# One bank per half for the first row of blocks of a seven-product GRU, and its moving sums in 256-column instructions

## The chip, the cores and the metric

The kernel runs on one core of one Trainium2 chip. The metric is the device time of one execution in microseconds. Kernels are compared by the median of several executions; a profile is one further execution, recorded by the hardware profiler.

## What is computed

Two graph layers run over 128 graphs of 128 nodes with 256 features, all in fp32. Layer 0 is a gated graph network: three steps with shared GRU weights. Layer 1 is one head of graph attention. Each is applied to a normalised input and added to it:

```python
h = jnp.maximum(_layernorm(x, axis=-1), 0.0)
for i in range(3):                       # layer 0
    m = jnp.einsum('bnd,de->bne', h, weight[i])
    aggr = jnp.einsum('bst,bsd->btd', A, m)
    gi = aggr @ w_ih.T + b_ih
    gh = h @ w_hh.T + b_hh
    r = jax.nn.sigmoid(i_r + h_r)
    z = jax.nn.sigmoid(i_z + h_z)
    n = jnp.tanh(i_n + r * h_n)
    h = (1.0 - z) * n + z * h
...
att = softmax(where(adj == 0, -inf, leaky_relu(s1[:, :, None] + s2[:, None, :])))   # layer 1
out = x + einsum('bij,bjo->bio', att, h @ W.T)
```

`gi` and `gh` are split in three parts (r, z, n), and `A` is `adj != 0`. The weights of `m` are multiplied into those of `gi` ahead of the steps, so that a step only aggregates `h` and applies the gates.

## The kernel before

**Tiles.** Four graphs make a group (G = 4), so there are 32 groups and 32 x 3 = 96 GRU steps. The state of a group is kept in columns: tile `hT` is [128 partitions, C = 2 chunks of features, T = 512 columns], where a column is a node. `aT` is the aggregated input in the same form. H = 256 is half of the columns.

**A step** (`gru_step`, L627) has two blocks: `blocks(0, ...)` makes the gate r and the hidden part of n, `blocks(1, ...)` the gate z and the given part of n. A block multiplies a 2 x 2 matrix of weight blocks (output half o, input half) by a 2 x 2 matrix of data blocks X11, X21 (first half of the columns, chunks 0 and 1) and X12, X22 (second half). It does so with seven products instead of eight, after Winograd. `moving_sums` (L441, instructions at L445, L448, L450 and L452) prepares the sums of data on VectorE, once for `hT` and once for `aT`: T1 = X12 - X11, T2 = X22 - T1, T3 = X22 - X12 and T4 = X22 - X21 - T1. The sums of weights S1 to S4 are made once per kernel.

`blocks` (L662) emits in this order, where each product (L636, matmul at L650) is three matmuls of 256 columns, each in two passes of TensorE:

1. `u` = W11 X11, which ScalarE copies to the first halves of `c1` (L670);
2. `m7` = S3 T3, which ScalarE copies to `m` (L673);
3. `u` += S2 T2, after which VectorE makes `c2 = u + m` (L676);
4. the first halves of `c1` += W12 X21, which completes C11;
5. `u` += S1 T1, which ScalarE copies to the second halves of `c1` (L680), and from which VectorE makes `c22 = u + m` (L684); only then is `u` free for the next block;
6. `c2` += N22 T4;
7. the second halves of `c1` += S4 X22, which completes C12.

`c1`, `c2`, `u` and `m7` are in PSUM. `c1` is [128, 2, 512]: one bank for each of the block's two results (q = 0, 1), in which the first half of the columns (C11) and the second (C12) stand side by side. Row o = 0 of the outcome is read from it, both halves in one instruction of 512 columns: r by `reset` (tanh, L701), the hidden part by `state_half` (L708), z by `update` (L734), all on ScalarE, and the given part by `add_half` on VectorE (L741, v += c1). Row o = 1 lies in `c2` and `c22` and is read in instructions of 256 columns at the same lines. `candidate` (L598) then makes v = (r + 1) v, and `state` (L606 to L614) a tanh and three sums on VectorE for each chunk, which give the new `hT`.

**Other work.** `gathered` (L566) multiplies by the adjacency (`pa`) or by the attention (`pq`); `to_rows` (L483) transposes on TensorE. `epilogue` (L803) is the attention of a finished group: norm statistics (L406), scores (`junk`, L840), softmax (L883 to L899), the product with `W` (`po`, L944) and the final sum (L951). For all but the last two groups it turns its tiles by VectorE transposes and small DMAs (`tq`, L827; `prT`). All DMAs are issued from SP (L60).

**What sets the order.** The order on each engine is fixed when the program is built. A planner (class `Order`, L169) keeps a time for each engine at which it is free; every piece of work is a generator that yields an engine, a length and the time at which its inputs are ready. `product` puts its matmuls and then calls `fill`, which issues what fits on the other engines until the product's end, and `matmuls`, which adds up to 1 us of other TensorE work. `finish` runs what must be done first. Two groups are in work alternately (lanes), and `gru_step` returns its two `state` tasks, which the next step, of the other lane, finishes at `order.finish(last)`, after the sixth product of its second block. Lengths that the planner takes are constants in the code. At run time [...] each engine works its list off in order.

Of the kernel before, what the change touches and what calls it, by code (L numbers as in the profile page):

```python
# [14 lines left out]
P = 128  # L15
# [12 lines left out]
def preln_gnn_kernel(  # L28
# [110 lines left out]
    c1 = ps_sum.tile([P, 2, T], F32, name="c1")  # L139
# [3 lines left out]
    for bank in (c1[:, 0, :], c1[:, 1, :], c2.rearrange("p g t -> p (g t)")):  # L143
        put(nc.tensor.matmul(bank, zero[:, 0:P], zero, start=True, stop=True))
# [294 lines left out]
    T1, D1, T2, T4, T3 = range(5)  # L439

    def moving_sums(X, into, ready, name):  # L441

        yield DVE2, 0.36, ready
        t = work.tile([P, 5, H], F32, tag=f"t{name[0]}", name=f"t_{name}")
        put(nc.vector.tensor_tensor(t[:, T3, :], X[:, 1, H:T], X[:, 0, H:T], ALU.subtract))  # L445
        into[T3] = t, order.free[DVE]
        into[T1] = t, (yield DVE2, 0.62, ready)
        put(nc.vector.tensor_tensor(t[:, T1 : D1 + 1, :], X[:, :, H:T], X[:, :, 0:H], ALU.subtract))  # L448
        into[T2] = t, (yield DVE2, 0.36, ready)
        put(nc.vector.tensor_tensor(t[:, T2, :], X[:, 1, H:T], t[:, T1, :], ALU.subtract))  # L450
        into[T4] = t, (yield DVE2, 0.36, ready)
        put(nc.vector.tensor_tensor(t[:, T4, :], t[:, D1, :], t[:, T1, :], ALU.subtract))  # L452
# [174 lines left out]
    def gru_step(s, last):  # L627
# [34 lines left out]
        def blocks(no, gates):  # L662

            m = gate.tile([P, 2, H], F32, tag="m", name=f"m_{name}_{no}")
            c22 = gate.tile([P, 2, H], F32, tag="c22", name=f"c22_{name}_{no}")
            done = product(gates, lambda q: u[:, q, :], W11, (0, 0), None, banks["u"], True, (ACT,))
            t = order.take(ACT, 0.57, max(done, banks["c1"]))
            put(nc.scalar.copy(c1[:, :, 0:H], u))  # L670
            done = product(gates, lambda q: m7[:, q, :], S3, None, T3, 0.0, True, (ACT,))
            tm = order.take(ACT, 0.57, done)
            put(nc.scalar.copy(m, m7))  # L673
            done = product(gates, lambda q: u[:, q, :], S2, None, T2, t, False, (DVE,))
            t = order.take(DVE, 0.62, max(done, tm, banks["c2"]))
            put(nc.vector.tensor_tensor(c2, u, m, ALU.add))  # L676
            product(gates, lambda q: c1[:, q, 0:H], W12, (1, 0), None)
            done = product(gates, lambda q: u[:, q, :], S1, None, T1, t, False, (ACT,))
            t = order.take(ACT, 0.57, done)
            put(nc.scalar.copy(c1[:, :, H:T], u))  # L680

            order.fill(t, (DVE,))
            tc22 = banks["u"] = order.take(DVE, 0.62, t)
            put(nc.vector.tensor_tensor(c22, u, m, ALU.add))  # L684
            done = product(gates, lambda q: c2[:, q, :], N22, None, T4, 0.0, False, (ACT, DVE))
            yield c22, tc22, done
            done = product(
                gates, lambda q: c1[:, q, H:T], S4, (1, 1), None, t, False, (ACT, DVE)
            )
            yield c22, tc22, done  # L690
# [3 lines left out]
        c22, t22, done = next(phase)  # L694
# [4 lines left out]
        def reset(o, cols, src, length, ready):  # L699
            t = order.take(ACT, length, ready)  # L700
            put(nc.scalar.activation(  # L701
                r[:, o, cols], src, AF.Tanh, bias=brz[:, o : o + 1], scale=0.5
            ))
            return t

        def state_half(o, cols, src, length, ready):
            t = order.take(ACT, length, ready)
# [4 lines left out]

        low, high, full = slice(0, H), slice(H, T), slice(0, T)
        reset(1, high, c22[:, 0, :], 0.38, t22)
        reset(1, low, c2[:, 0, :], 0.38, done)
        banks["c2"] = state_half(1, low, c2[:, 1, :], 0.38, done)
        _, _, done = next(phase)
        reset(0, full, c1[:, 0, :], 0.6, done)
        banks["c1"] = state_half(0, full, c1[:, 1, :], 0.6, done)
        t1 = state_half(1, high, c22[:, 1, :], 0.38, t22)  # L720
        s.v_ready = [0.0, 0.0]
        half_task = order.add(0, candidate(s, r, v, (banks["c1"], t1)))
# [3 lines left out]
        c22, t22, done = next(phase)  # L726
# [5 lines left out]
        def update(o, cols, src, length, ready):  # L732
            t = order.take(ACT, length, ready)
# [5 lines left out]
        def add_half(o, cols, src, length, ready):  # L739
            t = order.take(DVE, length, max(ready, s.v_ready[o]))  # L740
            put(nc.vector.tensor_tensor(v[:, o, cols], v[:, o, cols], src, ALU.add))  # L741
            return t

        add_half(1, high, c22[:, 1, :], 0.38, t22)
        update(1, high, c22[:, 0, :], 0.38, t22)
        tv = add_half(1, low, c2[:, 1, :], 0.38, done)
        banks["c2"] = update(1, low, c2[:, 0, :], 0.38, tv)
# [336 lines left out]
```

## Time and profile before

| | us |
|---|---|
| median of 3 runs | 2203.93 (2202.45 to 2205.67) |
| the profiled execution | 2205.54 |
| its span, first to last instruction | 2203.8 |
| TensorE (PE) busy | 2176.6 |
| VectorE (DVE) busy | 1744.5 |
| ScalarE (ACT) busy | 1309.3 |
| GpSimd (POOL) busy | 103.3 |
| mean granted clock of TensorE | 0.997 of full speed |

A group line of the profile names the source line, engine, operation, output <- inputs with their sizes, and the count, then busy us and mean ns of one, then the engine's idle time before and what ended it. A line of the waits names who waited for whom, us in total, times, and the longest. A line of the timeline has the start, the length, the engine and the instruction, with the idle time before it in brackets. Ends of matmuls are modelled: two passes in a row look as if they overlapped, so distances are taken between starts. "c" stands for all of `c1`, `c2`, `c22`, because numbers are left out of names.

### The profile page before, as it was taken

What the parts mean: (1) busy time and instruction counts of PE and PEld (TensorE: products, weight loads), DVE (VectorE), ACT (ScalarE), POOL (GpSimd) and SP (SyncE); (2) the same over time, 40 slices, a digit from 0 to 9 for tenths busy, and PEclk for the clock granted to TensorE, in tenths of its full rate; (3) what the DMA queues carried; (4) which work ended last, traced back from release to release, by engine and by line L of the source; (5) the groups of instructions that cost most, each with busy time, mean ns of one, the idle gap of its engine ahead of it and who ended that gap; (6) DMA issues with size and microseconds to landing.
All of it is one profiled execution on the core that took longest, in us unless ns stands there. A gap on an engine that the chain in (4) does not pass through costs nothing.

```text
span 2203.8 us, 32865 instructions
## 1 busy us (share of the span) xinstructions
PE 2176.6 (99%) x11259; PEld 1931.5 (88%) x11259; DVE 1744.5 (79%) x3960; ACT 1309.3 (59%) x2694; POOL 103.3 (5%) x204
## 2 busy tenths in 40 slices
PE   8999999999999999999999999999999999999997
PEld 7888888888888888888888888888888888888886
DVE  7678777788788878787888787887787888887866
ACT  5566656556566566656566565665655665656654
POOL 1000000000000000000000000000000000000000
PEclk9999999999999999999999999999999999999998
DMA  4001130131212212022210312213022021221101
GB/s 134 1 15 30 30 67 11 31 76 21 56 33 56 48 32 50 25 55 51 52 31 29 61 41 54 53 22 71 20 53 45 20 58 37 56 44 36 33 20 34
DMA packets 380936, 93.24 MB, mean 42 GB/s; under 512 B 325216, under 2 KB 376672, under 8 KB 380768
## 3 DMA queue, kind: packets, MB, share of 16 engines
q1 hardware_dynamic: 380768, 91.13, 19.1%
q8 instruction: 89, 1.46, 0.3%
q14 instruction: 79, 0.65, 0.1%
HBM read 35.92 MB, written 16.84 MB: 24 GB/s over the span
## 4 chain that ended last, share of the span: by engine, by line
PE 91%; DVE 4%; SPq 3%; DMA 1%; ACT 1%; issue 1%; DVEq 0%; ACTq 0%
PE u L650 31%; PE c L650 31%; PE m L650 10%; PE pa L566 7%; PE po L944 4%; SPq L60 3%; PE pq L566 3%; PE pr L483 2%; DMA xt<-in_x 1%; PE pw L348 1%; DVE v L741 1%; ACT z L734 0%; DVE c L684 0%; DVE hT L610 0%; DVE hT L608 0%
## 5 line engine op out<-in xcount | busy, mean ns | idle before, releaser
L650 PE MATMUL u<-t_h,s_hh 128*128 128x256 f32 x1152 | 343.5, 380 | 2.0 <-ACT c L670 2.0
L650 PE MATMUL u<-t_a,s_f 128*128 128x256 f32 x1152 | 311.3, 379 | 0.0
L650 PE MATMUL c<-aT,s_f 128*128 128x256 f32 x1152 | 311.3, 379 | 0.0
L680 ACT COPY c<-u 128x512 f32<-128x512 f32 x192 | 109.4, 570 | 325.8 <-PE u L650 294.3
L650 PEld LDWEIGHTS c<-aT,s_f 128*128 128x128 f32 x1152 | 218.9, 190 | 29.7
L650 PEld LDWEIGHTS u<-t_a,s_f 128*128 128x128 f32 x1152 | 218.9, 190 | 29.7
L650 PEld LDWEIGHTS u<-t_h,s_hh 128*128 128x128 f32 x1152 | 211.9, 190 | 33.8 <-ACT c L670 4.3
L741 DVE TENSOR_TENSOR v<-v,c 128x256 f32<-128x256 f32 (+1 forms) x288 | 139.5, 509 | 126.5 <-ACT z L734 121.5
L734 ACT ACTIVATE z<-c,brz 128x256 f32<-128x256 f32 (+1 forms) x288 | 159.8, 556 | 116.5 <-DVE c L684 67.4
L650 PE MATMUL c<-hT,s_hh 128*128 128x256 f32 x768 | 228.5, 379 | 0.0
L676 DVE TENSOR_TENSOR c<-u,m 128x512 f32<-128x512 f32 x192 | 134.3, 700 | 114.6 <-PE u L650 98.8
L701 ACT ACTIVATE r<-c,brz 128x256 f32<-128x256 f32 (+1 forms) x288 | 151.2, 552 | 91.8 <-DVE c L684 61.8
L684 DVE TENSOR_TENSOR c<-u,m 128x512 f32<-128x512 f32 x192 | 131.8, 687 | 69.2 <-ACT c L680 67.9
L673 ACT COPY m<-m 128x512 f32<-128x512 f32 x192 | 112.6, 587 | 100.4 <-PE m L650 100.4
L650 PE MATMUL m<-t_h,s_hh 128*128 128x256 f32 x576 | 171.5, 379 | 0.0
L650 PE MATMUL c<-t_h,s_hh 128*128 128x256 f32 x576 | 171.4, 379 | 0.0
L670 ACT COPY c<-u 128x512 f32<-128x512 f32 x192 | 111.3, 580 | 85.7 <-DVE v L741 71.9
L650 PEld LDWEIGHTS c<-hT,s_hh 128*128 128x128 f32 x768 | 144.7, 190 | 19.0
L590 ACT COPY aT<-pa 128x512 f32<-128x512 f32 x192 | 109.2, 584 | 84.6 <-PE pa L566 84.5
L650 PE MATMUL m<-t_a,s_f 128*128 128x256 f32 x576 | 156.1, 380 | 0.7 <-DVE t_a L445 0.7
L650 PE MATMUL u<-aT,s_f 128*128 128x256 f32 x576 | 155.6, 379 | 0.0
L650 PE MATMUL c<-t_a,s_f 128*128 128x256 f32 x576 | 155.6, 379 | 0.0
(122 smaller groups left out, 4188.0 us busy)
## 6 DMA issues: line engine op xcount, KB each, us to landing
xt<-in_x SPq DMA_DIRECT2D x31, 512.0 KB
out<-xt SPq DMA_DIRECT2D x31, 512.0 KB
tq<-hT SPq DMA_DIRECT2D x480, 32.0 KB
hT_a<-tq_a SPq DMA_DIRECT2D x448, 32.0 KB
at<-in_adj SPq DMA_DIRECT2D x32, 256.0 KB
e<-line SPq DMA_DIRECT2D x30, 256.0 KB
prT<-e SPq DMA_DIRECT2D x480, 16.0 KB
line<-turned SPq DMA_DIRECT2D x120, 0.5 KB
```

The source lines that it names most:

```text
L566: put(nc.tensor.matmul(pa[:, k * P : (k + 1) * P], h[:, k, c * P : (c + 1) * P], A[:, k, :], start=True, stop=True,))
L590: put(nc.scalar.copy(aT[:, c, :], pa))
L650: put(nc.tensor.matmul(to(q), S[0][:, gate_no, weight, :], moving, start=first and q == 0 and i == 0, stop=(i == len(ends) - 1), skip_grou ...
L670: put(nc.scalar.copy(c1[:, :, 0:H], u))
L673: put(nc.scalar.copy(m, m7))
L676: put(nc.vector.tensor_tensor(c2, u, m, ALU.add))
L680: put(nc.scalar.copy(c1[:, :, H:T], u))
L684: put(nc.vector.tensor_tensor(c22, u, m, ALU.add))
L701: put(nc.scalar.activation(r[:, o, cols], src, AF.Tanh, bias=brz[:, o : o + 1], scale=0.5))
L734: put(nc.scalar.activation(z[:, o, cols], src, AF.Tanh, bias=brz[:, C + o : C + o + 1], scale=0.5))
L741: put(nc.vector.tensor_tensor(v[:, o, cols], v[:, o, cols], src, ALU.add))
L944: put(nc.tensor.matmul(po[:, j, :], hs[:, c, k * P : (k + 1) * P], gwt[:, c, :], start=(c == 0), stop=(c == C - 1),))
```

## The change

`c1` becomes two PSUM tiles of one bank each, by half of the columns: `c1[0]` holds C11 and `c1[1]` holds C12, for both results. `blocks` yields once more, after the fourth product, and `c1[0]` is read there; `c1[1]` is read after the seventh. All reads of row o = 0 are 256 columns now. For the second half, the sum on VectorE stands ahead of the tanh of z. `order.finish(last)` and `order.finish([half_task])` come after the fourth product instead of the sixth. In `moving_sums` T4 is made as T2 - X21, D1 = X22 - X21 is gone, and the four sums are instructions of 256 columns in the order T3, T1, T2, T4. The planner's lengths for them are 0.34, and 0.38 for every read.

```diff
@@ -136,11 +136,12 @@
 
     zero = borrowed(gate, [P, C, T], "r", "zero", T, bufs=1).bitcast(mybir.dt.bfloat16)[:, 0:T]
     put(nc.vector.memset(zero, 0.0))
-    c1 = ps_sum.tile([P, 2, T], F32, name="c1")
+    c1 = [ps_sum.tile([P, 2, H], F32, name=f"c1_{n}") for n in range(2)]
     c2 = ps_sum.tile([P, 2, H], F32, name="c2")
     u = ps_sum.tile([P, 2, H], F32, name="u")
     m7 = ps_sum.tile([P, 2, H], F32, name="m7")
-    for bank in (c1[:, 0, :], c1[:, 1, :], c2.rearrange("p g t -> p (g t)")):
+    for bank in (*c1, c2):
+        bank = bank.rearrange("p g t -> p (g t)")
         put(nc.tensor.matmul(bank, zero[:, 0:P], zero, start=True, stop=True))
...
 
-    T1, D1, T2, T4, T3 = range(5)
+    T1, T2, T3, T4 = range(4)
 
     def moving_sums(X, into, ready, name):
 
-        yield DVE2, 0.36, ready
-        t = work.tile([P, 5, H], F32, tag=f"t{name[0]}", name=f"t_{name}")
-        put(nc.vector.tensor_tensor(t[:, T3, :], X[:, 1, H:T], X[:, 0, H:T], ALU.subtract))
-        into[T3] = t, order.free[DVE]
-        into[T1] = t, (yield DVE2, 0.62, ready)
-        put(nc.vector.tensor_tensor(t[:, T1 : D1 + 1, :], X[:, :, H:T], X[:, :, 0:H], ALU.subtract))
-        into[T2] = t, (yield DVE2, 0.36, ready)
-        put(nc.vector.tensor_tensor(t[:, T2, :], X[:, 1, H:T], t[:, T1, :], ALU.subtract))
-        into[T4] = t, (yield DVE2, 0.36, ready)
-        put(nc.vector.tensor_tensor(t[:, T4, :], t[:, D1, :], t[:, T1, :], ALU.subtract))
+        t = work.tile([P, 4, H], F32, tag=f"t{name[0]}", name=f"t_{name}")
+        x11, x21, x12, x22 = (X[:, c, n * H : (n + 1) * H] for n in range(2) for c in range(2))
+        for i, one, other in ((T3, x22, x12), (T1, x12, x11), (T2, x22, t[:, T1]), (T4, t[:, T2], x21)):
+            into[i] = t, (yield DVE2, 0.34, ready)
+            put(nc.vector.tensor_tensor(t[:, i, :], one, other, ALU.subtract))
...
@@ -666,18 +662,19 @@
             m = gate.tile([P, 2, H], F32, tag="m", name=f"m_{name}_{no}")
             c22 = gate.tile([P, 2, H], F32, tag="c22", name=f"c22_{name}_{no}")
             done = product(gates, lambda q: u[:, q, :], W11, (0, 0), None, banks["u"], True, (ACT,))
-            t = order.take(ACT, 0.57, max(done, banks["c1"]))
-            put(nc.scalar.copy(c1[:, :, 0:H], u))
+            t = order.take(ACT, 0.57, max(done, banks["c1_0"]))
+            put(nc.scalar.copy(c1[0], u))
             done = product(gates, lambda q: m7[:, q, :], S3, None, T3, 0.0, True, (ACT,))
             tm = order.take(ACT, 0.57, done)
             put(nc.scalar.copy(m, m7))
             done = product(gates, lambda q: u[:, q, :], S2, None, T2, t, False, (DVE,))
             t = order.take(DVE, 0.62, max(done, tm, banks["c2"]))
             put(nc.vector.tensor_tensor(c2, u, m, ALU.add))
-            product(gates, lambda q: c1[:, q, 0:H], W12, (1, 0), None)
+            done = product(gates, lambda q: c1[0][:, q, :], W12, (1, 0), None)
+            yield done
             done = product(gates, lambda q: u[:, q, :], S1, None, T1, t, False, (ACT,))
-            t = order.take(ACT, 0.57, done)
-            put(nc.scalar.copy(c1[:, :, H:T], u))
+            t = order.take(ACT, 0.57, max(done, banks["c1_1"]))
+            put(nc.scalar.copy(c1[1], u))
 
             order.fill(t, (DVE,))
             tc22 = banks["u"] = order.take(DVE, 0.62, t)
@@ -685,75 +682,81 @@
             done = product(gates, lambda q: c2[:, q, :], N22, None, T4, 0.0, False, (ACT, DVE))
             yield c22, tc22, done
             done = product(
-                gates, lambda q: c1[:, q, H:T], S4, (1, 1), None, t, False, (ACT, DVE)
+                gates, lambda q: c1[1][:, q, :], S4, (1, 1), None, t, False, (ACT, DVE)
             )
-            yield c22, tc22, done
+            yield done
 
...
         phase = blocks(0, [(0, (hid, given)), (2, (hid,))])
-        c22, t22, done = next(phase)
+        low, high = slice(0, H), slice(H, T)
+        done = next(phase)
...
-        def reset(o, cols, src, length, ready):
-            t = order.take(ACT, length, ready)
+        def reset(o, cols, src, ready):
...
-        def state_half(o, cols, src, length, ready):
-            t = order.take(ACT, length, ready)
+        def state_half(o, cols, src, ready):
...
-        low, high, full = slice(0, H), slice(H, T), slice(0, T)
-        reset(1, high, c22[:, 0, :], 0.38, t22)
-        reset(1, low, c2[:, 0, :], 0.38, done)
-        banks["c2"] = state_half(1, low, c2[:, 1, :], 0.38, done)
-        _, _, done = next(phase)
-        reset(0, full, c1[:, 0, :], 0.6, done)
-        banks["c1"] = state_half(0, full, c1[:, 1, :], 0.6, done)
-        t1 = state_half(1, high, c22[:, 1, :], 0.38, t22)
+        reset(0, low, c1[0][:, 0, :], done)
+        banks["c1_0"] = state_half(0, low, c1[0][:, 1, :], done)
+        c22, t22, done = next(phase)
+        reset(1, high, c22[:, 0, :], t22)
+        reset(1, low, c2[:, 0, :], done)
+        banks["c2"] = state_half(1, low, c2[:, 1, :], done)
+        done = next(phase)
+        reset(0, high, c1[1][:, 0, :], done)
+        banks["c1_1"] = state_half(0, high, c1[1][:, 1, :], done)
+        t1 = state_half(1, high, c22[:, 1, :], t22)
         s.v_ready = [0.0, 0.0]
-        half_task = order.add(0, candidate(s, r, v, (banks["c1"], t1)))
+        half_task = order.add(0, candidate(s, r, v, (banks["c1_1"], t1)))
 
 
         phase = blocks(1, [(1, (hid, given)), (2, (given,))])
-        c22, t22, done = next(phase)
+        done = next(phase)
         order.finish([half_task])
         order.finish(last)
...
-        def update(o, cols, src, length, ready):
-            t = order.take(ACT, length, ready)
+        def update(o, cols, src, ready):
...
-        def add_half(o, cols, src, length, ready):
-            t = order.take(DVE, length, max(ready, s.v_ready[o]))
+        def add_half(o, cols, src, ready):
+            t = order.take(DVE, 0.38, max(ready, s.v_ready[o]))
             put(nc.vector.tensor_tensor(v[:, o, cols], v[:, o, cols], src, ALU.add))
             return t
 
-        add_half(1, high, c22[:, 1, :], 0.38, t22)
-        update(1, high, c22[:, 0, :], 0.38, t22)
-        tv = add_half(1, low, c2[:, 1, :], 0.38, done)
-        banks["c2"] = update(1, low, c2[:, 0, :], 0.38, tv)
+        t = update(0, low, c1[0][:, 0, :], done)
+        banks["c1_0"] = add_half(0, low, c1[0][:, 1, :], t)
+        c22, t22, done = next(phase)
+        add_half(1, high, c22[:, 1, :], t22)
+        update(1, high, c22[:, 0, :], t22)
+        tv = add_half(1, low, c2[:, 1, :], done)
+        banks["c2"] = update(1, low, c2[:, 0, :], tv)
         s.halves = []
         new = columns_tile("hT", name)
         first = order.add(0.5, state(s, 1, hT, new, v, z, tv))
-        _, _, done = next(phase)
-        t = update(0, full, c1[:, 0, :], 0.6, done)
-        t = banks["c1"] = add_half(0, full, c1[:, 1, :], 0.62, t)
+        done = next(phase)
+        t = add_half(0, high, c1[1][:, 1, :], done)
+        banks["c1_1"] = update(0, high, c1[1][:, 0, :], t)
         return [first, order.add(0.5, state(s, 0, hT, new, v, z, t))]
 
-    banks = dict.fromkeys(("u", "c1", "c2"), 0.0)
+    banks = dict.fromkeys(("u", "c1_0", "c1_1", "c2"), 0.0)
 
```

More of the change, by code (lines that the diff above doesn't have):

```diff
@@ L697, in gru_step @@
         v = gate.tile([P, C, T], F32, tag="v", name=f"v_{name}")
-        def reset(o, cols, src, length, ready):
-            t = order.take(ACT, length, ready)
+        def reset(o, cols, src, ready):
+            t = order.take(ACT, 0.38, ready)
             put(nc.scalar.activation(
@@ L704, in reset @@
             return t
-        def state_half(o, cols, src, length, ready):
-            t = order.take(ACT, length, ready)
+        def state_half(o, cols, src, ready):
+            t = order.take(ACT, 0.38, ready)
             put(nc.scalar.activation(
@@ L730, in gru_step @@
         z = gate.tile([P, C, T], F32, tag="z", name=f"z_{name}", bufs=1)
-        def update(o, cols, src, length, ready):
-            t = order.take(ACT, length, ready)
+        def update(o, cols, src, ready):
+            t = order.take(ACT, 0.38, ready)
             put(nc.scalar.activation(
```

## The prediction

> **What bounds the kernel now.** I read the page's shares first, then the waits, then the timeline around the longest waits of TensorE, then the tail. Part 1 of the page:
>
> ```profile
> PE 2176.6 (99%) x11259; PEld 1931.5 (88%) x11259; DVE 1744.5 (79%) x3960; ACT 1309.3 (59%) x2694; POOL 103.3 (5%) x204
> ```
>
> TensorE is never free for long, and the timeline shows its pace: a 256-column pass starts every 0.216 us (two in 0.43), a 128-column one every 0.108. The diff leaves all its passes in place, so only the time between them can change. Taking starts of neighbouring passes and subtracting these paces, I find 10.6 us lost between 24 and 2160 us. Before 24 us the kernel waits for its first loads, which stay where they are; after the last product (2162.3 us) comes a tail of 41.5 us up to 2203.8. Here are the waits (total us, times, longest):
>
> ```profile
> ACT c L670 <- DVE v L741: 71.9, 89, 1.1
> PEld u L650 <- DVE c L684: 5.4, 5, 1.7
> PE u L650 <- ACT c L670: 2.0, 5, 0.4
> PEld m L650 <- DVE t_a L445: 2.3, 4, 0.6
> ```
>
> The large first line costs TensorE almost nothing; the three small ones are its losses. One of the five bad places, in the timeline of all engines (start, length):
>
> ```profile
> 1800.04 1.03 PE L650 MATMUL c<-aT,s_f 128*128 128x256 f32 x4
> 1800.05 0.43 DVE L406 BATCH_NORM_STATS2 st_a<-xt 128x6 f32<-128x256 f32 x1 [2.44 <-DMA xt<-in_x]
> ...
> 1801.47 0.68 DVE L684 TENSOR_TENSOR c<-u,m 128x512 f32<-128x512 f32 x1
> ...
> 1802.21 0.70 PE L650 MATMUL u<-hT,s_hh 128*128 128x256 f32 x2 [1.14 <-DVE c L684]
> ...
> 1804.07 0.69 DVE L741 TENSOR_TENSOR v<-v,c 128x512 f32<-128x512 f32 x1 [1.12 <-ACT z L734]
> 1804.47 0.59 PE L650 MATMUL m<-t_h,s_hh 128*128 128x256 f32 x2
> 1804.84 0.57 ACT L670 COPY c<-u 128x512 f32<-128x512 f32 x1 [0.81 <-DVE v L741]
> ...
> 1805.46 0.70 PE L650 MATMUL u<-t_h,s_hh 128*128 128x256 f32 x2 [0.40 <-ACT c L670]
> ```
>
> VectorE stands 2.44 us before a row load; the second sum (L684) is queued behind it, and `u` is freed late: the four passes from 1800.04 end at 1800.90 by pace, the next starts at 1802.21, so **1.31 us**. Then a second loss: the copy L670 may not overwrite `c1` until L741 has read all of it, L741 waits for the 512-column `z` (L734), and TensorE, due at 1804.90, starts at 1805.46: **0.56 us**. After either stop the first pass takes 0.10 us more. The five places (458, 994, 1262, 1691, 1801) lose 0.49+0.34+0.63+1.41+1.31 = 4.2 us at the first stop and 5 x 0.56 = 2.8 at the second, with restarts 8.0. Four have a row load in front, the one at 1691 the returning state (`xt<-xt,tq`, L827). The rest: four late first sums of `aT` (L445), 4 x 0.43 = 1.7; small ones, 0.8. Together 10.6.
>
> [...] L684's copy was done 2.4 us before it ran. [...]
>
> **The change, part by part.** There are 96 steps.
> 1. *Moving sums.* L448 (512 columns, 684 ns) becomes a 256-column one (about 419 ns, L445): 0.265 us less, 192 times, 51 us of VectorE. The dependence changes: T4 follows T2. That order can't delay a product: T4's consumer is the sixth. S3, which needs T3, still gets it first, so the four losses at L445 aren't addressed; T2 comes up to 0.27 us sooner.
> 2. *Halved reads.* Each of L701, L708, L734 splits a 512-column read (687, 681, 687 ns) in two (484, 485, 491): +0.28, +0.29, +0.30 us, 96 times, 83 us of ScalarE (59% becomes 63%). L741 gains 2 x 419 - 688 = 0.15, 14 us. VectorE is then 1744 - 51 + 14 = 1707. Both lie under TensorE's matmuls, and cost zero while these last; bare, the adds would be 97 us.
> 3. *The early read.* The first half of `c1` is read after the fourth product instead of the seventh. The copy that begins the next block then finds its bank free: the 71.9 us of ScalarE waiting goes, and so does the second stop, 2.8 + 0.5 of restarts = 3.3 us. What is next late there: the copy now follows `z` of the second half, at 256 columns. From L684's end: two adds 0.76, the third to 1.15, `z` to 1.8, copy to 2.4; S2 is due at 2.6. Covered.
> 4. *New waits.* In the built program ScalarE's early tanh stands before the second copy of `u`, and VectorE's early add before L684. Behind them wait the copy, L684, and then TensorE at `u`. W12 ends 1.3 us before S1; tanh and add take 0.48+0.42 with some 0.1 of hand-over, or 0.97 for both of ScalarE's reads in the first block. They fit. If the cover were gone, 0.1 to 1 us a block; below nothing is excluded, as they only add. I take zero. The previous state must also be finished two products (2.6 us) sooner; it still has a whole block of products (9.1 us) and four more for some 4.2 us of VectorE, so zero.
> 5. *The planner.* With other costs it lays out everything anew. POOL and SP have the same number of instructions, TensorE the same 5924; the order differs. Counting TensorE passes in program order between a row load and its first statistics: before, six loads have only 3.0 us of passes, four of which are the stops at 458, 994, 1262 and 1801; loads with 3.9 or more never waited. After, one has 3.0, one 3.5, ten have 3.9, the others more. So I take one such stop as left, 0.5 us, instead of 4.2; the range is 0 to 5, as L827 has more places at 2.2 to 2.6 (twelve, seven before, one of which stopped TensorE). With 1.2 for L445 and 0.6 of small ones, **2.3 of 10.6 us stay**: -8.3.
> 6. *The tail.* Up to the end of the last `hT` sums nothing gets shorter: TensorE waits for `prT`, whose 16 issues on SP stand at the same point of the last products. Then VectorE is the chain:
>
> ```profile
> 2167.43 0.69 DVE L614 SCALAR_TENSOR_TENSOR hT<-hT,v 128x512 f32<-128x512 f32 x1
> ...
> 2179.94 0.69 DVE L894 TENSOR_REDUCE nm<-e 128x4 f32<-128x512 f32 x1
> ...
> 2183.83 3.79 PE L566 MATMUL pq<-prT,h_b 128*128 128x128 f32 x16 [0.68 <-ACT prT L912]
> ...
> 2195.60 0.38 PE L908 MATMUL pp<-ident,e 128*128 128x128 f32 x2
> ```
>
> Before, the maximum of group 30 (L894) ends 2180.63. In the built order of after, group 31's additions and statistics stand ahead and wait for the transposes (about 0.7 idle), and its first four score products (4 x 0.47) come before group 30's softmax. From `hT` (about 2168.5, 0.4 later since `z` now follows the add): 0.7 idle, 0.7+1.2+0.2+0.7+0.9 for group 31, 1.7 for four L951, 3.8 for eight products, 1.9 for the four, 0.3, and 2.4 for L883 to L894: 2183.0 to 2183.7, near 3 us late. The softmax of 31's first half directly follows, which used to come later. TensorE's `pq` starts near 2187.2, then 3.4 (half pace after idle, as at 2183.83), some 1.3, and three `po` of 1.75: L908 near 2197.5 to 2198 against 2195.60. The rest is alike. I take **+2.4** (+1 to +4).
>
> **The sum**, against the profiled execution's span: 2203.8 - 8.3 + 2.4 = 2197.9. That run took 2205.54, 1.74 around its span. The runs shown have their median, 2203.93, 1.6 below it; the same difference of -5.9 gives 2198.0.
>
> **Rivals.**
> *The stops move.* Only the second stop goes (-3.3); row loads and L827 stop VectorE elsewhere for as much. For it: the queue is still in order and SP as busy. Against it: the 3.9 us distances. 2203.93 - 3.3 + 2.4 = 2203.
> *Slower: `prT` comes too late.* At eleven softmaxes in the middle, the built order has only 2.4 us of passes from the last `prT` issue to `pq` (L566); before, never under 4.3 but in the tail. The issue takes 0.65, landing 1.58 more (both from the tail); in before SP ran 0.9 to 2.4 behind program order at such places. With a lag over 0.2 it decides, and at 1.0 to 1.2 each stop costs about 1 us with restart: 2198 + 11 = 2209. Against: with 5.0 the gap was still 3.0 to 3.4, and the planner keeps a reserve for the landing.
> *The tail costs nothing*, as some of VectorE's work moved ahead would have ended the chain anyway: 2195.6.
> *The change does nothing* is excluded for part 3 by the built order; for the time it falls under the first rival.
>
> **How the numbers follow.** Forecast 0.60 (2194.5 to 2201.5), stops move 0.22, `prT` late 0.09, free tail 0.09. About 0.2%, 4.4 us, is what a measurement here can tell from no change: under 2199.5 is faster, over 2208.3 slower. Four fifths of the forecast, the free tail and a little of the second case are faster: 0.60; slower 0.09; same 0.31. The range 2193.5 to 2205.5 leaves out the late `prT` and a little of each end.
>
> **What would show it.** After: no wait of L670's successor on L741; VectorE near 1707, ScalarE near 1392 us; one or two stops of TensorE at `u`; last product near 2154; a tail of 43 to 45 us. Wrong if `pq` waits for `prT` in the middle, if sums of `aT` stop TensorE more than four times, or if stops at `u` repeat with the order's period.

## The result, and the profile after

| | before | after |
|---|---|---|
| median | 2203.72 us (6 runs, 2202.45 to 2206.58) | 2195.81 us (6 runs, 2195.55 to 2198.21) |
| profiled execution, its span | 2205.54, 2203.8 us | 2198.21, 2196.2 us |
| last product ends | 2162.3 us | 2152.4 us |
| from there to the end | 41.4 us | 43.9 us |

The ratio of the medians is 0.9963 (95% interval 0.9951 to 0.9976): 8 us faster, where 5.9 were forecast. Line numbers after the change are a few lower or higher than before: matmul L646, copies of `u` L666 and L677, second sum L681, reads of `c1` L699, L706, L734 and L741, last state sum L610.

Part 1 of the page of the changed kernel:

```profile
PE 2174.2 (99%) x11259; PEld 1935.3 (88%) x11259; DVE 1720.7 (78%) x4056; ACT 1378.6 (63%) x2982; POOL 120.4 (5%) x204
```

The passes of TensorE are the same in number; VectorE has less to do and ScalarE more. The waits of the changed kernel (total us, times, longest):

```profile
ACT c L666 <- PE u L646: 32.2, 98, 0.8
...
DVE st_a L407 <- DMA xt<-in_x: 3.3, 2, 2.3
```

The copy that begins a block (L666) waits for its product alone; the 71.9 us behind L741 are gone. VectorE's waits for row loads have fallen to 3.3 us, of which 2.3 are one wait among the first loads. TensorE's waits at `u` for the second sum, 5.4 and 3.4 us before, are 0.2 us in all. The window of the changed kernel from 24 us to the last product (window, its length, busy time of each engine, TensorE's clock, DMA share, GB/s):

```profile
24.00:2152.50 2128.50, 2128.50 (x11068) 1899.88 (x11068) 1678.67 (x3912) 1351.80 (x2913) 111.57 (x183) 1.00 0.19 40
```

By the modelled ends TensorE is busy without a gap for 2128 us; before, 2132.1 of 2138.3. The place that answers to the one shown of before is the one tight row load that is left (all engines):

```profile
328.25 0.43 DVE L407 BATCH_NORM_STATS2 st_a<-xt 128x6 f32<-128x256 f32 x1 [1.02 <-DMA xt<-in_x]
...
329.93 0.69 PE L646 MATMUL u<-hT,s_hh 128*128 128x256 f32 x2
...
331.52 0.59 ACT L666 COPY c<-u 128x512 f32<-128x512 f32 x1
...
332.61 0.59 PE L646 MATMUL u<-t_h,s_hh 128*128 128x256 f32 x2
```

VectorE stands 1.02 us before the load. The first pass on `u` at 329.93 is still on time, and only the one behind it comes 0.10 us late. The copy starts at once, and the next passes on `u` at 332.61 keep the pace: no second stop.

**One measure for all that follows.** I take the distances between starts of neighbouring passes of TensorE, subtract the pace (0.216 us for 256 columns, 0.108 for 128) and sum what is left in three stretches: *start* (up to 24 us), *middle* (to the last product) and *tail* (behind it, passes of 128 columns 0.213 us apart among it). Span minus the three sums is 2166.5 to 2166.8 us in every kernel of this study, so differences of the sums account for differences of the spans to 0.3 us. The three sums of a row come from one profiled execution. The changed kernel, e4 and e8 are built alike up to the last product and lose 0.5, 0.5 and 1.9 us there, so a difference of 1.4 us in the middle can arise without any change of the program.

| kernel | median us | ratio to before (95%) | start | middle | tail |
|---|---|---|---|---|---|
| before | 2203.7 to 2204.2 | | 7.7 | 10.6 | 18.9 |
| after | 2195.81 | 0.9963 (0.9951 to 0.9976) | 7.8 | 0.5 | 21.4 |
| e1 before, new sums, old lengths | 2204.14 | 1.0000 (0.9991 to 1.0008) | 7.3 | 10.5 | 17.9 |
| e2 before, row loads earlier | 2204.61 | 1.0000 (0.9992 to 1.0009) | 6.4 | 8.9 | 20.0 |
| e3 after, old sums | 2196.37 | 0.9960 (0.9948 to 0.9973) | 7.1 | 2.5 | 18.4 |
| e4 after, last epilogue planned 2.0 us later | 2197.01 | 0.9963 (0.9950 to 0.9977) | 7.2 | 0.5 | 21.3 |
| e5 before, both landings earlier | 2199.34 | 0.9979 (0.9973 to 0.9986) | 6.3 | 5.0 | 20.1 |
| e6 after, first tile read late | 2209.11 | 1.0026 (1.0016 to 1.0035) | 7.3 | 15.9 | 17.7 |
| e7 as e6, both landings earlier | 2199.80 | 0.9979 (0.9973 to 0.9986) | 7.4 | 10.0 | 14.0 |
| e8 after, last epilogue planned 3.0 us later | 2196.77 | 0.9970 (0.9959 to 0.9982) | 6.9 | 1.9 | 19.6 |
| e9 before, new sums, their own order | 2206.94 | 1.0015 (1.0009 to 1.0022) | 6.6 | 10.7 | 20.6 |
| e10 after, HOP 0.15 | 2193.82 | 0.9955 (0.9943 to 0.9968) | 6.0 | 2.9 | 15.8 |
| e11 before, HOP 0.15 | 2196.54 | 0.9967 (0.9954 to 0.9979) | 7.0 | 5.4 | 15.6 |
| e12 after, row loads earlier, last epilogue 3.0 us later | 2196.57 | 0.9968 (0.9955 to 0.9980) | 7.2 | 0.3 | 21.3 |

A first stop is one of TensorE at the first pass on `u` of a block, a second stop one at the first pass of S2 in that block, where the copy of `u` is late. A restart is the 0.10 us more that the pass behind a stop takes. A landing is the moment when a DMA's data are there; the planner's reserve is the time from issue to landing that it counts on. "Split" means `c1` in two tiles. "Distance" is the TensorE passes, in us, that the built order puts between a DMA's issue and its first reader.

### The profile page after: what moved, and what is told of

Read it like the earlier page. It is cut to its first block, busy times and chain, and to the rows that moved or that the text cites. A ratio compares the mean times of both kernels' runs of the same rounds, so it can differ in the third digit from the quotient of the medians.

```text
span 2196.2 us, 33240 instructions
## 1 busy us (share of the span) xinstructions
PE 2174.2 (99%) x11259; PEld 1935.3 (88%) x11259; DVE 1720.7 (78%) x4056; ACT 1378.6 (63%) x2982; POOL 120.4 (5%) x204
## 4 chain that ended last, share of the span: by engine, by line
PE 98%; DVE 1%; SPq 0%; DMA 0%; ACT 0%; issue 0%; POOL 0%; POOLq 0%; DVEq 0%; ACTq 0%
PE u L646 34%; PE c L646 34%; PE m L646 11%; PE pa L562 8%; PE po L947 5%; PE pq L562 3%; PE pr L479 3%; PE pw L349 1%; SPq L60 0%; DVE junk L843 0%; DMA wih<-in_w_ih_t 0%; PE pt_a L457 0%; PE pp L911 0%; DMA prT<-e 0%; DVE xt L954 0%
## 5 line engine op out<-in xcount | busy, mean ns | idle before, releaser
L646 PE MATMUL u<-t_h,s_hh 128*128 128x256 f32 x1152 | 343.0, 379 | 0.3 <-DVE c L672 0.3
L734 ACT ACTIVATE z<-c,brz 128x256 f32<-128x256 f32 x384 | 185.4, 483 | 240.8 <-DVE v L741 95.9
L646 PE MATMUL u<-t_a,s_f 128*128 128x256 f32 x1152 | 311.3, 379 | 0.0
L646 PE MATMUL c<-aT,s_f 128*128 128x256 f32 x1152 | 311.3, 379 | 0.0
L699 ACT ACTIVATE r<-c,brz 128x256 f32<-128x256 f32 x384 | 176.3, 478 | 193.6 <-PE c L646 109.3
L741 DVE TENSOR_TENSOR v<-v,c 128x256 f32<-128x256 f32 x384 | 154.3, 420 | 164.0 <-ACT z L734 114.5
L672 DVE TENSOR_TENSOR c<-u,m 128x512 f32<-128x512 f32 x192 | 134.2, 699 | 145.3 <-PE u L646 138.7
L646 PEld LDWEIGHTS u<-t_a,s_f 128*128 128x128 f32 x1152 | 218.9, 190 | 29.7
L646 PEld LDWEIGHTS c<-aT,s_f 128*128 128x128 f32 x1152 | 218.9, 190 | 29.7
L646 PEld LDWEIGHTS u<-t_h,s_hh 128*128 128x128 f32 x1152 | 216.1, 190 | 29.7 <-DVE c L672 1.4
L646 PE MATMUL c<-hT,s_hh 128*128 128x256 f32 x768 | 228.5, 379 | 0.0
L677 ACT COPY c<-u 128x512 f32<-128x512 f32 x192 | 109.4, 570 | 118.5 <-PE u L646 115.8
L706 ACT ACTIVATE v<-c,bhn 128x256 f32<-128x256 f32 x384 | 172.5, 478 | 0.0
L646 PE MATMUL m<-t_h,s_hh 128*128 128x256 f32 x576 | 171.5, 379 | 0.0
L646 PE MATMUL c<-t_h,s_hh 128*128 128x256 f32 x576 | 171.3, 379 | 0.0
L681 DVE TENSOR_TENSOR c<-u,m 128x512 f32<-128x512 f32 x192 | 131.6, 685 | 42.3 <-ACT c L677 42.0
L646 PEld LDWEIGHTS c<-hT,s_hh 128*128 128x128 f32 x768 | 142.6, 190 | 17.6
L646 PE MATMUL u<-aT,s_f 128*128 128x256 f32 x576 | 155.7, 379 | 0.0
L646 PE MATMUL m<-t_a,s_f 128*128 128x256 f32 x576 | 155.7, 379 | 0.0
L646 PE MATMUL c<-t_a,s_f 128*128 128x256 f32 x576 | 155.6, 379 | 0.0
```

The lines of the kernel that those rows point to most:

```text
L646: put(nc.tensor.matmul(to(q), S[0][:, gate_no, weight, :], moving, start=first and q == 0 and i == 0, stop=(i == len(ends) - 1), skip_grou ...
L677: put(nc.scalar.copy(c1[1], u))
L699: put(nc.scalar.activation(r[:, o, cols], src, AF.Tanh, bias=brz[:, o : o + 1], scale=0.5))
L706: put(nc.scalar.activation(v[:, o, cols], src, AF.Identity, bias=bhn[:, o : o + 1], scale=0.5))
L734: put(nc.scalar.activation(z[:, o, cols], src, AF.Tanh, bias=brz[:, C + o : C + o + 1], scale=0.5))
```

## The experiments

**Which part of the change gains? (e1, e9, e3)** e1 gives the old kernel the new sums but leaves the planner the old lengths:

```diff
-        put(nc.vector.tensor_tensor(t[:, T1 : D1 + 1, :], X[:, :, H:T], X[:, :, 0:H], ALU.subtract))
...
+        for i, one, other, cost in ((T3, x22, x12, 0.36), (T1, x12, x11, 0.62), (T2, x22, t[:, T1], 0.36), (T4, t[:, T2], x21, 0.36)):
+            into[i] = t, (yield DVE2, cost, ready)
+            put(nc.vector.tensor_tensor(t[:, i, :], one, other, ALU.subtract))
```

> The kernel before with the new moving sums alone; the planner is told the old costs, so that its order stays nearly that of before (six row loads again with 3.0 us of TensorE passes ahead of their statistics). My theory (what was gained are TensorE's stops behind row loads, with their second stops at c1, and VectorE's work itself lies hidden): VectorE's busy time falls by some 51 us to 1693, the five stops and the five second stops stay, time 2203 (2201 to 2205). The rival that less work on VectorE is the gain: 2196 to 2199.

Measured: 2204.14 us, no difference. The lengths of VectorE's instructions sum to 50.4 us less (its busy time, which counts overlaps once, falls by 32), and the middle still loses 10.5 us, at the same places: VectorE meets the same five landings and waits 1.4 to 2.0 us for the four row loads, where it was 1.6 to 2.4 (at 994 us the first stop falls out, the second of 0.56 stays). Less work on VectorE is not the gain.

e9 tells the planner the new lengths too; it is the diff's `moving_sums` alone, in the old kernel (here against e1):

```diff
-        for i, one, other, cost in ((T3, x22, x12, 0.36), (T1, x12, x11, 0.62), (T2, x22, t[:, T1], 0.36), (T4, t[:, T2], x21, 0.36)):
-            into[i] = t, (yield DVE2, cost, ready)
+        for i, one, other in ((T3, x22, x12), (T1, x12, x11), (T2, x22, t[:, T1]), (T4, t[:, T2], x21)):
+            into[i] = t, (yield DVE2, 0.34, ready)
```

> The kernel before with the new moving sums and their new costs told to the planner, which lays out an order of its own: 14 row loads with 3.2 us of passes (one in each 137 us), returning states with 2.2. c1 stays in one tile. My theory (shorter sums gain nothing; the one tile makes each stop cost 0.56 us more): as in the kernel before or worse, first stops of 0.2 to 0.8 us at most of the 14 places, each with a second of 0.56: 2207 (2201 to 2214). The rival that the sums gain once the planner knows them: 2200 or less.

Measured: 2206.94 us. The time was foreseen, its reason was not: no first stop comes from the row loads at 3.2 us. The middle loses 10.7 us in other small pieces, once in each 134 us: 13 first sums of `aT` 0.33 us late, 18 copies of `u` mostly 0.07 us late, and the restarts of 0.10 behind them and elsewhere.

e3 leaves the split and takes the sums back:

```diff
-        for i, one, other in ((T3, x22, x12), (T1, x12, x11), (T2, x22, t[:, T1]), (T4, t[:, T2], x21)):
...
+        put(nc.vector.tensor_tensor(t[:, T1 : D1 + 1, :], X[:, :, H:T], X[:, :, 0:H], ALU.subtract))
...
+        put(nc.vector.tensor_tensor(t[:, T4, :], t[:, D1, :], t[:, T1, :], ALU.subtract))
```

> The changed kernel with the old moving sums: two tiles by half, read when complete, remain. The planner's order is a third one: 14 row loads with 3.5 us of passes ahead of their statistics, one with 1.7. My theory (the distance of the row loads decides the first stop, the split banks take away only the second): some 0.2 to 0.3 us at each of the 14 and 2 at the one, no second stops, the softmax of group 30 ahead of group 31 in the tail: 2199 (2195 to 2203). The rival that the split and early read carry the whole gain: 2194 to 2196. The rival that the shorter sums carry it: 2202 or more.

Measured: 2196.37 us, as the changed kernel. From 46 us to the last product TensorE loses 0.1 us. The time is in the range given, but the mechanism forecast was wrong: the row loads at a distance of 3.5 us (twelve in the built order, where 14 had been counted) and one of 1.7 never stop it, so the distance alone does not decide. The moving sums are not needed for the gain.

**Does the old kernel need anything but earlier loads? (e2, e5)**

```diff
-        into[g] = load(g), t + LAND + 1.5
+        into[g] = load(g), t + LAND + 6.0
```

> The kernel before; only the planner's reserve for a row load's landing is raised from LAND + 1.5 to LAND + 6.0. c1 and the sums are as before. In the built order the least row load in the middle then has 4.8 us of passes ahead of its statistics. My theory (the stops come from the distance of the row loads, the second stop is only a consequence of the first): the stops at row loads go and take their second stops along, 2.8 + 2.2 + 0.8 of the 10.6 us, so 2198 (2196 to 2201), and the wait of the copy of u on L741 stays in the list of waits while costing TensorE little. The rival that the second stop needs the split banks: 2201 or more. The rival that any new order loses as much elsewhere: 2203.

Measured: 2204.61 us, no gain. The row loads' stops are gone, as foreseen. Others have come: at 864, 1266 and 1668 us the returning state (`tq`, L827) now stops VectorE. The timeline of e2:

```profile
1663.76 1.29 DVE L827 TENSOR_TENSOR xt<-xt,tq 128x512 f32<-128x512 f32 x2 [3.10 <-DMA tq<-hT]
...
1670.39 0.70 PE L650 MATMUL u<-hT,s_hh 128*128 128x256 f32 x2 [1.91 <-DVE c L684]
...
1673.02 0.57 ACT L670 COPY c<-u 128x512 f32<-128x512 f32 x1 [0.81 <-DVE v L741]
```

From 1663.76 on VectorE works without a gap, statistics and all, and reaches L684 5.9 us later, 2.07 us too late for TensorE. The prediction's rival "the stops move" is seen at work here, on the old kernel. Each of the three first stops (0.10, 0.52 and 2.07 us) draws a second of 0.56: its size does not depend on the first.

e5 raises the reserve of the returning state as well:

```diff
-        return rows_.rearrange("p c (g f) -> p g c f", g=G), t + LAND
+        return rows_.rearrange("p c (g f) -> p g c f", g=G), t + LAND + 3.0
...
-        into[g] = load(g), t + LAND + 1.5
+        into[g] = load(g), t + LAND + 6.0
```

> The kernel before; the planner's reserves for both landings are raised: for a row load from LAND + 1.5 to LAND + 6.0, for the returning state from LAND to LAND + 3.0. c1 in one tile and the old sums stay. In the built order the row loads then have at least 4.8 us of passes ahead, the returning states in the middle 3.9 or 4.3 instead of 2.6. My theory (VectorE caught behind a landing is the one cause, and the second stop and the late sums of aT follow from the first): all three kinds vanish though c1 is not split, losses after 24 us fall under 3 us, and the time is near that of the changed kernel, 2196.5 (2194.5 to 2198.5). The rival that the split itself is needed, or that stops only move: 2201 or more.

Measured: 2199.34 us. Half of the middle's loss goes with `c1` in one tile, so the first half of my theory holds. The rest of it does not: four late first sums of `aT` (0.33 us and restart) stay, three of them with no stop ahead, so they do not follow from the stops. One first stop of 0.16 us is left, and it draws its second of 0.56.

**Does the early read matter, or only the two tiles? (e6, e7)** In e6 the first tile is read behind the seventh product:

```diff
-        reset(0, low, c1[0][:, 0, :], done)
-        banks["c1_0"] = state_half(0, low, c1[0][:, 1, :], done)
         c22, t22, done = next(phase)
...
         done = next(phase)
+        reset(0, low, c1[0][:, 0, :], done)
+        banks["c1_0"] = state_half(0, low, c1[0][:, 1, :], done)
         reset(0, high, c1[1][:, 0, :], done)
```

(and the same for `update` and `add_half` in the second block.)

> The changed kernel with two tiles and halved reads, but the first tile is read behind the seventh product instead of behind the fourth. The planner's order is another one, with 12 row loads at 1.7 to 2.2 us of passes. My theory (no early read, tight loads: first stops return, and the copy of u finds its bank still in use behind each): first stops of some 0.5 to 1.5 us at most of the 12 places, with a second stop of 0.2 to 0.6 behind each, 2207 (2202 to 2214). The rival that halved reads and two banks alone carry the gain: 2195 to 2197.

Measured: 2209.11 us, slower than before. VectorE stands 0.4 to 2.8 us at 12 row loads. First stops are fewer than I thought (three at L681, 1.5 us, and one of 1.9 at L672), but copies of `u` stop TensorE 25 times, 8.5 us. The timeline of e6 behind a first stop of 0.17 us:

```profile
736.56 0.75 DVE L741 TENSOR_TENSOR v<-v,c 128x256 f32<-128x256 f32 x2 [0.91 <-ACT z L734]
...
738.42 0.70 PE L646 MATMUL u<-t_h,s_hh 128*128 128x256 f32 x2 [0.65 <-ACT c L666]
```

The copy (at 737.78) must wait until L741 has read the first tile, as before the change, and TensorE starts 0.81 us late. In this order two tiles and halved reads gain nothing without the early read.

e7 takes the landings out of it, with e6's late read and both reserves raised:

```diff
-        return rows_.rearrange("p c (g f) -> p g c f", g=G), t + LAND
+        return rows_.rearrange("p c (g f) -> p g c f", g=G), t + LAND + 2.0
...
-        into[g] = load(g), t + LAND + 1.5
+        into[g] = load(g), t + LAND + 6.0
```

> As the kernel with the late read, but with the planner's reserves raised (row loads LAND + 6.0, returning state LAND + 2.0): row loads at 5.2 us of passes or more, returning states at 4.3 or more in the middle. My theory: no first stop, so no second one, 2196 (2194 to 2199), although ScalarE waits for the late read again. The rival that the early read gains time by itself: 2200 or more.

Measured: 2199.80 us, but not for my reason: 4.9 us of its gain are a shorter tail, and the middle loses 10.0 us, twice what e5 loses with one tile, although VectorE waits only 1.5 us for DMA there. The time just misses the rival's 2200, but its mechanism is there: late reads cost by themselves, 0.30 us and a restart in each 134 us and small pieces beside. The timeline of e7 on ScalarE tells why:

```profile
1613.10 0.49 ACT L699 ACTIVATE r<-c,brz 128x256 f32<-128x256 f32 x1
...
1613.45 0.89 ACT L706 ACTIVATE v<-c,bhn 128x256 f32<-128x256 f32 x2
...
1614.21 0.62 ACT L666 COPY c<-u 128x512 f32<-128x512 f32 x1
```

The eight halved reads of a block stand together, from 1611.25 on, and the copy queues behind them: the last pass of the product that it copies starts at 1613.07, the copy at 1614.21, and TensorE's next pass on `u` is 0.30 us late. The early read also takes two of these reads out of this queue.

**Is it the order? (e10, e11)** Both kernels with one constant of the planner changed, `HOP` from 0.2 to 0.15; both then have an order of their own.

```diff
-    HOP = 0.2
+    HOP = 0.15
```

> The changed kernel; only the planner's time from engine to engine, HOP, is 0.15 instead of 0.2, which gives another order: two row loads in the middle with only 1.3 us of passes (and one with 1.7, one with 2.6). It brings first stops into the changed kernel. My theory (the early read takes the second stop away whatever the first): first stops of 1.5 to 2.8 us at the two places, behind them no stop of the fourth product over 0.15 us; 2200 (2197 to 2203). The rival that any first stop draws a second one: 0.5 us at the copy behind each.

Measured: 2193.82 us, the fastest of all. VectorE stands before eight row loads in the middle, 8.9 us in all, and TensorE hardly notices. The timeline of e10 at the longest:

```profile
1658.91 1.95 PE L562 MATMUL pa<-A,h 128*128 128x128 f32 x16
1658.92 0.43 DVE L407 BATCH_NORM_STATS2 st_a<-xt 128x6 f32<-128x256 f32 x1 [1.95 <-DMA xt<-in_x]
...
1660.08 0.68 DVE L672 TENSOR_TENSOR c<-u,m 128x512 f32<-128x512 f32 x1
...
1661.99 0.59 PE L646 MATMUL u<-t_h,s_hh 128*128 128x256 f32 x2
```

1.95 us of waiting cost nothing, because the sum behind them has 16 matmuls of `pa` (1.7 us at their pace) to hide in. What a wait costs was set, at the places shown, by what stands behind it in the queue, and by the TensorE work until that is due. So this run brought no large first stop, and was a poor test of the second. The one first stop at L681 (0.17 us, 1532) drew none.

> The kernel before; only HOP is 0.15. Another order: row loads with 5.6 us or more, returning states with 0.9 once and 2.2 to 2.6 seven times. My theory (with one tile any order loses at the landings, each with a second stop of 0.56, and at late sums of aT): 2203 (2200 to 2207). The rival that the changed kernel's gain is the luck of its order and another order of the kernel before finds it too: 2197 or less.

Measured: 2196.54 us, ratio 0.9967 (0.9954 to 0.9979). My theory falls here: another order of the *old* kernel, without any part of the change, is as fast as the changed one. It gets there by another way, though: its middle loses 5.4 us where the changed kernel's loses 0.5, and its tail 15.6 where that one's loses 21.4. The waits of e11:

```profile
ACT c L670 <- DVE v L741: 61.8, 81, 0.8
...
DVE st_a L406 <- DMA xt<-in_x: 2.4, 1, 2.4
...
PE pr L483 <- DVE hT L614: 2.1, 13, 0.2
```

The copy still waits 61.8 us for L741, and it costs TensorE 0.07 us and a restart in 2130 us. The one wait for a row load is at the start, those for the returning state are 0.7 us at most, and there is no first stop and no second behind one. Of the 5.4 us that the middle loses, 4.2 are 13 times 0.32 at transposes (`pr`) that wait for the last sum of a state. The split kernels, which finish the state two products sooner, have no such stop behind 46 us; that the one is the reason for the other was not tested. The tail is 3.3 us shorter than before. With the same constant the split kernel is 2.7 us faster by the medians (2192.83 to 2195.17 against 2195.4 to 2197.0). The two profiled spans lie 3.3 us apart: 2.5 in the middle and 1.0 at the start, less 0.2 in the tail.

**The tail (e4, e8, e12)** All three change how late the planner takes the last group's epilogue to be ready, by 2.0 us in e4 and 3.0 in e8 and e12; e12 has e2's earlier row loads beside:

```diff
-                    order.add(2, epilogue(s, p, max(s.halves)))
+                    order.add(2, epilogue(s, p, max(s.halves) + (2.0 if s.g == NG - 1 else 0.0)))
```

> The changed kernel; only the last group's epilogue is planned as ready 2.0 us later, so that the built order is the same up to the end of the last products, and behind it VectorE has the score products of group 30 ahead of group 31's work, as before. My theory (the 2.4 us in the tail are that order): 2193.4 (2193.0 to 2194.5), the tail 41.5 us instead of 43.8. The rival that they come from the later end of the state sums (z behind the add) and TensorE's half pace after idle time: at most 0.5 us back, 2195.3.

> The changed kernel; the last group's epilogue is planned as ready 3.0 us later. With 2.0 later VectorE still stood 2.55 us before the first addition of group 31; now all eight score products of group 30 precede it in the built order. The middle is unchanged. My theory (the 2.4 us of the tail are VectorE waiting for group 31's transposes ahead of group 30's score products): scores of group 30 start about 21.7 us behind the last product, the tail is 41.5 to 42.2, 2193.8 (2193.0 to 2194.6). The rival that group 31's second half sets the end in any order: 2195.3 or more.

> The changed kernel with both remaining edits: the row loads' reserve raised to LAND + 6.0 (least distance in the middle 3.9 instead of 3.0) and the last group's epilogue planned as ready 3.0 us later. My theory (1.3 us at the one tight row load, where the stop comes, and 1.7 in the tail): span 2193.8, time 2195.3 (2194.3 to 2196.2), about 1 us under the changed kernel. The rival that the last half group sets the end in any order: no difference, 2196.5.

Measured: 2197.01, 2196.77 and 2196.57 us: none is faster than the changed kernel, and the gains of 1 to 2.4 us that I expected did not come. The longest idle time of VectorE behind the last state sums (idle time in brackets), in the timeline of e4 and then in that of e12:

```profile
2160.30 0.69 DVE L827 TENSOR_TENSOR xt<-xt,pr_o 128x512 f32<-128x512 f32 x1 [2.55 <-PE pr_o L479]
```

```profile
2161.34 0.88 DVE L954 SCALAR_TENSOR_TENSOR xt<-po,rs,xt 128x256 f32<-128x256 f32 x2 [3.47 <-PE po L947]
```

One wait is replaced by another: with 2.0 us one addition of group 31 is still in front, with 3.0 the final sum of group 29 is, and TensorE delivers both late (in the changed kernel the 16 `pq` behind 3.43 us of idle time start about 0.213 us apart instead of 0.108). e8 has the built tail of e12 and a tail 1.6 us shorter (42.2 against 43.8): there the 16 `pq` behind the idle time took 2.78 us, at full pace at first, where the changed kernel's took 3.75.

e8 also gives what e10 did not, a large first stop in the split kernel, at the row load that the result above shows. VectorE stands 2.36 us there instead of 1.02:

```profile
328.77 0.43 DVE L407 BATCH_NORM_STATS2 st_a<-xt 128x6 f32<-128x256 f32 x1 [2.36 <-DMA xt<-in_x]
...
330.44 0.70 PE L646 MATMUL u<-hT,s_hh 128*128 128x256 f32 x2 [1.17 <-DVE c L681]
...
333.14 0.59 PE L646 MATMUL u<-t_h,s_hh 128*128 128x256 f32 x2
```

The first stop is 1.33 us. The copy starts at 332.04, and the pass on `u` at 333.14 is on pace. This is the one large first stop that any run with the early read shows. In e12, with that load earlier, the stop is gone (middle 0.3 us), which the time doesn't show.

## Why the prediction was right

The sum forecast was -8.3 in the middle and +2.4 in the tail; the profiled spans show -10.0 to the last product (2162.3 to 2152.4) and +2.4. By the steps of the prediction:

1. *Moving sums*: right. The sums are 418 to 425 ns each and take 50 us less. They gain nothing by themselves (e1), and the split gains without them (e3).
2. *Halved reads*: right. The lengths of VectorE's instructions sum to 36 us less (1938.2 to 1902.0), where 37 were forecast; the page's busy time falls by 24 only, because it counts overlapping ends once. ScalarE: 1378.6 against 1392, as the halved reads take 478 to 483 ns. That they cost zero holds only with the early read: in e7 the same reads, placed late, stop TensorE.
3. *The early read*: right in mechanism; the size was not measured by itself. The second stop was 0.56 us behind each first stop at L684 in the old kernel, whether that was 0.10 or 2.07 us long (before, e2, e5); it is 0.81 with a late read (e6) and absent with the early one behind a first stop of 1.33 (e8). But in the profile of the changed kernel hardly a first stop is left to draw a second, and e11 has none of either with one tile. So the new order alone would have taken the 5 x 0.56 with their restarts along, and the runs do not divide these 3.3 us between the order and the early read. In the profile of the changed kernel the early reads start 0.42 us or more after the start of the last pass of the fourth product, in all 96 steps. Most run beside passes of the fifth, into `u` (L699 in 94 steps, L706 in 95, L734 in 65, L741 in 66), and all end 1.0 us or more before the seventh begins. TensorE does not stop for them: the only passes beside them that come later than the pace are two restarts, of 0.10 us each. Whether half of a single tile could be read as early was not tried.
4. *New waits*: right, zero, as far as the middle shows (0.5 us in all). The first sum L672 was late twice by about 0.09 us.
5. *The planner*: right in direction, and the mis-sized term of the sum. I let 2.3 us of the 10.6 stay (1.2 for late sums of `aT`, 0.5 for one row load, 0.6 of small ones); 0.54 stayed. The late sums were taken to be untouched, as T3 still came first; they depend on the order, and in the new one they are on time, as they are in e11. The row load left at a distance of 3.0 us cost 0.10 us in the profiled run and 1.33 in e8's. My rule that 3.0 us stop and 3.9 do not is too coarse: 3.5 and even 1.7 did not (e3), nor did 1.95 us of waiting (e10).
6. *The tail*: the size came out as forecast, +2.4, the way there only in part. The changed kernel's lines that answer to the prediction's:

```profile
2160.60 0.69 DVE L827 TENSOR_TENSOR xt<-xt,pr_o 128x512 f32<-128x512 f32 x1 [2.21 <-PE pr_o L479]
...
2173.92 0.69 DVE L897 TENSOR_REDUCE nm<-e 128x4 f32<-128x512 f32 x1
...
2188.04 0.38 PE L911 MATMUL pp<-ident,e 128*128 128x128 f32 x2
```

The terms that the prediction lists from `pq` on, 2187.2 + 3.4 + 1.3 + 3 x 1.75, add up to 2197.2 and not to 2197.5 to 2198; so they forecast +1.6, and that +2.4 was met to a tenth is luck. VectorE waits 2.21 us for group 31's transposes, not 0.7. The maximum of group 30 comes 3.95 us later behind the last product than before (forecast near 3), `pq` 4.3 later, and the last `pp` 2.4 later, as more of group 31 was done by then. That this order is the cause was not shown: three other orders of the tail each met another wait.

**The rivals.** *The stops move* was wrong for the change and right for e2, where it took the whole gain. *`prT` too late*: in the changed kernel `pq` waits for `prT` once, in the tail, in spite of eleven distances of 2.4 us; e10, with 1.9 twice, has two stops at `pq` of 0.41 and 0.27 us, which fit (the profile names a landing of `tq` for the one and nothing for the other). *The tail costs nothing* was wrong. What no rival said is e11: an order of the old kernel gains 7 us by the medians. Of the 9.2 us between the profiled spans of before and e11, 5.2 are in the middle, 3.3 in the tail and 0.7 at the start. So about half of the 10 us that the change gained in the middle could be had by the order alone.

What stays open is the other half. The orders of the split kernel with the early read (after with e4 and e8; e12; e3; e10) lose 0.3 to 2.9 us in the middle, and the five of the old one (before with e1; e2; e5; e9; e11) 5.0 to 10.7. Whether an order of the old kernel exists that loses as little, the runs don't show. The early read frees ScalarE and the first tile sooner, which may widen the planner's room; that was not tested either. What the change is worth is thus 2.7 us beside one order of the old kernel and 8 beside another.

## What to carry to other kernels

Where a program's order is computed from lengths, a change is two changes, and a run of the old kernel under another order helps to tell them apart: here one constant gave the old kernel the same 0.3%. Compare by stages too, for that 0.3% came in good part from the tail, where the changed kernel had lost time. A wait on an in-order engine is priced by what is queued behind it and by the work that hides that, not by its length: 1.95 us cost nothing at one place and 1.02 us nearly nothing, while 2.44 us cost 1.31 and a second stop besides. When reads are halved, place one half elsewhere in time, or the halves can crowd the instruction that TensorE waits for, as in e7, where its pass on `u` came 0.30 us late.

## What the runs showed of the hardware

In the tail TensorE's 16 `pq` of 128 columns start about 0.213 us apart instead of 0.108 behind a stretch without work: behind 3.9 us from start to start before (at 2166.01, granted clock 0.52), behind 3.8 in the changed kernel (at 2155.95, granted clock 0.50). In e8, behind 3.2 us, the first nine of 16 kept the full pace; in e12, behind the same 3.2 us, none did. Their tails, built alike, differ by 1.6 us: 0.97 us arise at these 16 passes, and most of the rest at later passes of TensorE that were at half pace in e12 and less so in e8. In the middle of before, each of the 16 stops of TensorE at one of the seven products (0.08 to 1.41 us) is followed by one pass that takes 0.10 us more, and in e11 so is one of 0.07; behind the 13 stops of 0.32 us at transposes in e11 no such pass is seen.
